# Six gathers ahead in layer 2's mixtures, the loads of x and the sums in one loop, and sequence 0's attention norm behind the first addition

## The chip, the cores and the metric

The kernel runs on one core of one Trainium2 chip. A core has five engines with an instruction queue each: PE (TensorE, matrix products), DVE (VectorE), ACT (ScalarE), POOL (GpSimd) and SP (SyncE, which here only issues transfers). DMAs are issued from the queues of SP, ACT and POOL. An engine works off its queue in order; what one engine needs of another is a semaphore that it waits for. The metric is the device time of one execution in microseconds (us), lower is better. The kernel before was run three times: 1662.7, 1663.09 and 1671.05 us, median 1663.09.

## The reference

A stack of four "macaron" layers on x of 4 sequences x 512 tokens x 128 features, in float32. Each layer adds half of a feed-forward part, then an attention, then half of the same feed-forward part, each on the layer norm of x. Only layer 2 matters here. Its feed-forward part is a mixture of 8 experts in which the experts choose their tokens, and its attention is a linear one:

```python
# feed-forward: n_tok = 2048 tokens, E = 8 experts, k = 256 tokens for each expert
Sm = softmax(xf @ Wr + br)                # (tokens, experts)
G_t, idx_t = top_k(Sm.T, k)               # each expert takes its 256 best tokens
tokens = xf[idx]                          # (256, 8, 128)
mid = silu(einsum('keh,ehf->kef', tokens, W_up[e // 2]) + b_up[e // 2])   # 341 wide
out = einsum('kef,efh->keh', mid, W_down) + b_down
y = zeros_like(xf).at[idx].add(G[..., None] * out)

# attention: q, k = elu(.) + 1, 16 heads of 8
kv = einsum('bshd,bshe->bhde', k, v)
out = einsum('bshd,bhde->bshe', q, kv)
out = einsum('bse,fe->bsf', out.reshape(B, S, E), Wo) + bo

# layer 2
x = x + 0.5 * ffn(norm(x))
x = x + attn(norm(x))
x = x + 0.5 * ffn(norm(x))
```

A token can be taken by several experts, so the results are summed per token.

## The kernel before

x stays in SBUF as 128 partitions x 4 sequences x 4 tiles x 128 features for the whole kernel. Layers 0 to 3 follow each other; layer 2 is the calls `l2_ffn(0)`, `l2_attn()`, `l2_ffn(1)`.

`l2_ffn(k)` (L1165 to L1366), the mixture:

- For each of the 4 sequences it norms x on DVE, transposes the normed tiles on PE, multiplies with the router, and stores x itself to a memory tensor, `sums_of[k, 0]` (L1188, SP's queue). A second tensor, `sums_of[k, 1]`, was filled with zeros long before (`l2_clear`). The results of a token are added to one or the other of these two: they are the two half-sums.
- The normed rows, with the token's 8 probabilities halved behind the 128 features, are stored to memory as `xd` (L1200; the halving is POOL's instruction L1197).
- A search in 15 steps on DVE and PE finds each expert's threshold; then the places of the chosen tokens become the indices `idx` (L1278 to L1295).
- The expert loop. `fetch(e)` (L1304) gathers expert e's 256 rows in two indirect DMAs (h = 0 and 1) from `xd` into tiles `xg`, issued by POOL (L1308). `turn` transposes them on PE (`pt`) and copies them out on DVE (`xTe`, L1322), `up_` multiplies with the up matrix (`pu`) and takes silu on ACT (`mid`), `down` multiplies with the down matrix (`pdn`), adds the bias and scales by the probability on DVE (`y`, L1341 and L1343). Then two indirect DMAs add the two halves of the result to the two half-sums in memory, row by row (L1344, POOL): h = 0 to the first, h = 1 to the second. Two additions to the same half-sum may not overlap, so each waits until the one before it on that tensor has landed.
- The loop is a pipeline over e: `turn(e)`, `up_(e - 1)`, `down(e - 2)`. `AHEAD` experts are fetched before it; from then on `fetch(e)` is placed behind the additions of expert e - `AHEAD`, by a dependence that only orders POOL's queue (L1309 to L1314). `xg` has 16 buffers, one for every gather, `y` has 4, `xTe` and `mid` 3 each.
- At the end, for each sequence, SP loads the first half-sum into x (L1363), ACT's queue loads the second into a tile `yt` (L1362), and DVE adds them (L1366).

`l2_attn()` (L1369 to L1431): `begin(b)` norms sequence b on DVE (four statistics, four aggregates, an inverse root by small instructions on 128x4 numbers, four scalings `xn`), transposes it on PE (`ps`) and copies it out on ACT (`xT`), and adds the output bias to x on POOL (L1386). `project(b)` makes k, v and q with PE, DVE and ACT; `leave(b)` forms the product of keys and values, masks it to the heads on DVE (`kvm`), multiplies it with q (`po`), copies (`oT`, ACT), projects out (`pf`) and adds to x (L1419).

The program is written as loops, and a scheduler places the instructions of each engine into its queue by priorities and expected times; it keeps the data dependences and the added ones. A pool of tiles that is opened where another was closed takes over its memory, and its instructions wait for the last uses of the old tiles.

Of the kernel before, what the change touches and what calls it, by code (L numbers as in the profile page):

```python
# [14 lines left out]
ALU = mybir.AluOpType  # L15
# [5 lines left out]
B, S, D = 4, 512, 128  # L21
# [62 lines left out]
def kernel(  # L84
# [7 lines left out]
    nc = tc.nc  # L92
# [35 lines left out]
    x = res.tile([P, B, TT, D], F32, tag="x", name="x")  # L128
# [5 lines left out]
    def take(t, cols, name):  # L134
        at, n = cols[name]
        return t[:, at : at + n]
# [61 lines left out]
    def over_tiles(row):  # L198
        return row.unsqueeze(1).to_broadcast([P, TT, D])
# [964 lines left out]

    def l2_ffn(k):  # L1165
        W = D + NE
        with tc.tile_pool(name=f"l2f{k}", bufs=1, reuse_waits="tile") as wk:
# [132 lines left out]
            bup = take(pcl, PCOL, "bup")  # L1300
            AHEAD = 4
            xg, xTs, mids, added = {}, {}, {}, {}
# [48 lines left out]
            for e in range(NE + 2):  # L1351
                if e < NE:
                    turn(e)
                if 0 <= e - 1 < NE:
                    up_(e - 1)
                if 0 <= e - 2 < NE:
                    down(e - 2)
                    if e - 2 + AHEAD < NE:
                        fetch(e - 2 + AHEAD)
            for b in range(B):  # L1360
                y = wk.tile([P, TT, D], F32, tag="yt", bufs=B, name=f"yt2_{k}_{b}")
                nc.scalar.dma_start(out=y, in_=sums_of[k, 1][b * S : (b + 1) * S, :].rearrange("(t p) d -> p t d", p=P))  # L1362
                nc.sync.dma_start(  # L1363
                    out=x[:, b], in_=sums_of[k, 0][b * S : (b + 1) * S, :].rearrange("(t p) d -> p t d", p=P)
                )
                nc.vector.tensor_tensor(x[:, b], x[:, b], y, op=ALU.add)  # L1366


    def l2_attn():  # L1369
        with tc.tile_pool(name="l2a", bufs=2, reuse_waits="tile") as wk:  # L1370
# [9 lines left out]

            xTs, qs, ks, vs = {}, {}, {}, {}

            def begin(b):
                xn = layer_norm(wk, x[:, b], f"a2_{b}")
                xTs[b] = transposed(wk, xn, f"a2_{b}")
                nc.gpsimd.tensor_tensor(x[:, b], x[:, b], over_tiles(take(rws, ROW, "bo2")), op=ALU.add)  # L1386

# [32 lines left out]

            begin(0)
            begin(1)
            project(0)
            for b in range(B):
# [432 lines left out]
    for e in range(NE):  # L1857
        t = wexp3.tile([P, N_E3], F32, tag="we3", name=f"we3_{e}")
        nc.sync.dma_start(out=t, in_=e_pack[e * P : (e + 1) * P, :])
        we3.append(t)  # L1860
    l2_ffn(0)
    l2_attn()
    l2_ffn(1)
    early.close()
# [162 lines left out]
```

## Time and profile before

| what | us |
|---|---|
| median of 3 runs | 1663.09 |
| profiled execution, its own time | 1666.47 |
| its span | 1664.7 |
| first mixture, search and indices (from 871.5) to the first gather | 40.9 |
| first mixture, first gather (912.4) to the first addition to memory (926.7) | 14.3 |
| first mixture, first addition to memory to the end of the last one's issue (968.4) | 41.7 |
| loads of x and the half-sum, to DVE's first addition (975.0) | 6.6 |
| attention, first addition to the last L1419 (1016.6) | 41.5 |
| second mixture, first gather (1073.2) to the first addition to memory (1087.7) | 14.5 |
| second mixture, additions to memory (to 1128.9) | 41.2 |
| loads, to DVE's first addition (1135.2) | 6.3 |

The profile is of one execution on the core. Times in its rows are microseconds from the start of the span unless marked ns; "[4.58 <-DVE y L1343]" at the end of a row means that the engine stood idle for 4.58 us before it and that the last thing it waited for was DVE's write of y in line 1343; "issue" is idle time for which the profile shows no releaser. Line numbers are those of the kernel of that profile.

Over the whole span PE is busy 81%, DVE 62%, ACT 40% and POOL 35%. These are averages over stages with different limits, and layer 2 takes about a sixth of the span (from the first mixture's norms at 854 to its last additions into x at 1138).

### The profile page before, as it was taken

How to read it: one execution, taken by the hardware profiler on the slowest of the kernel's cores; microseconds unless marked ns; L12 is line 12 of the kernel's file. 1: busy time of each engine (PE TensorE's matmuls, PEld its weight loads, DVE VectorE, ACT ScalarE, POOL GpSimd, SP SyncE). 2: the span in 40 equal slices, each digit the busy share in tenths (PEclk: the TensorE clock that was granted, in tenths of full speed). 3: DMA queues.
4: the chain of work that ended last, by engine and by line, in shares of the span. 5: the costliest groups of instructions: out<-in, count | busy, mean ns of one | idle time of the engine just before them, and what ended most of it. 6: DMA issues, size and time to landing. Idle time of an engine off the chain costs nothing.

```text
span 1664.7 us, 24721 instructions
## 1 busy us (share of the span) xinstructions
PE 1355.9 (81%) x8372; PEld 849.3 (51%) x8372; DVE 1025.0 (62%) x3179; ACT 668.1 (40%) x1413; POOL 582.6 (35%) x811
## 2 busy tenths in 40 slices
PE   3999899999899987979983646363885899998685
PEld 2898533443698633434552534252784233334685
DVE  4547787787446678888757267625214788883311
ACT  1433477777423323333320212020342377775242
POOL 0354265450255252222210730171784110100585
PEclk9999899999899998989985867585897699998698
DMA  8022212120311010004021221023643422311445
GB/s 322 26 67 59 47 51 64 45 54 17 123 61 49 22 52 1 1 1 190 14 64 30 40 60 53 11 37 82 213 150 100 95 60 57 66 33 28 121 167 183
DMA packets 97144, 121.26 MB, mean 73 GB/s; under 512 B 12223, under 2 KB 85428, under 8 KB 95481
## 3 DMA queue, kind: packets, MB, share of 16 engines
q1 hardware_dynamic: 76393, 69.84, 14.8%
q0 software_dynamic: 15968, 44.98, 9.1%
q10 hardware_dynamic: 4656, 4.86, 0.9%
q8 instruction: 66, 1.08, 0.3%
q14 instruction: 61, 0.50, 0.1%
HBM read 91.88 MB, written 27.79 MB: 72 GB/s over the span
## 4 chain that ended last, share of the span: by engine, by line
PE 64%; DVE 14%; DMA 7%; POOL 6%; issue 5%; SPq 2%; ACT 2%; POOLq 0%; DVEq 0%; ACTq 0%
PE pa L162 9%; PE po L162 7%; PE av L162 7%; PE smax L162 6%; PE sexp L162 6%; PE pc L162 6%; PE pb L162 4%; PE p3b L162 3%; PE lg L162 2%; PE p3a L162 2%; DMA sum<-y,idx 2%; PE p L162 2%; POOL y L1608 2%; PE pq L162 1%; DVE mp L718 1%
## 5 line engine op out<-in xcount | busy, mean ns | idle before, releaser
L718 DVE TENSOR_REDUCE mp<-smax 128x1 f32<-128x512 f32 (+1 forms) x512 | 326.7, 684 | 57.3 <-PE smax L162 56.4
L756 ACT ACTIVATE e<-sexp 128x512 f32<-128x512 f32 x512 | 271.3, 599 | 99.5 <-PE sexp L162 98.4
L162 PE MATMUL smax<-keys,queries 72*128 72x512 bf16 x512 | 200.6, 403 | 11.4 <-DMA queries<-rows_q 4.6
L162 PE MATMUL sexp<-queries,keys 75*128 75x512 bf16 (+1 forms) x512 | 193.1, 388 | 6.2 <-DMA queries<-mT 4.5
L162 PEld LDWEIGHTS <-th 128*128 128x128 bf16 x768 | 74.0, 96 | 97.4 <-issue 4.8
L543 ACT ACTIVATE gl<-pa 128x256 f32<-128x256 f32 x160 | 61.3, 383 | 154.8 <-PE pa L162 115.0
L162 PEld LDWEIGHTS <-queries 72*128 72x128 bf16 x512 | 51.9, 102 | 134.3 <-issue 82.3
L1557 POOL DMA_INDIRECT xg<-xd,src x46 | 46.8, 1018 | 175.3 <-DVE wi L1547 168.1
L544 DVE TENSOR_TENSOR hid<-pa,gl 128x256 f32<-128x256 f32 x160 | 67.3, 422 | 58.7 <-ACT gl L543 58.4
L162 PE MATMUL po<-we,hid 128*128 128x128 f32 x768 | 91.7, 276 | 0.0
L162 PEld LDWEIGHTS po<-we,hid 128*128 128x128 f32 x768 | 90.7, 192 | 1.9
L610 POOL DMA_INDIRECT yg<-y,idx x64 | 66.6, 1040 | 52.5 <-DMA y<-y 42.1
L162 PE MATMUL pa<-ei,we 128*128 128x256 f32 (+1 forms) x352 | 82.7, 390 | 1.5 <-DVE x L910 0.8
L162 PE MATMUL pa<-xTe,we 128*128 128x256 f32 (+1 forms) x352 | 81.8, 381 | 1.0 <-DVE xTe L532 1.0
L162 PEld LDWEIGHTS <-keys 75*128 75x128 bf16 (+1 forms) x512 | 50.2, 100 | 57.7 <-issue 15.5
L162 PEld LDWEIGHTS pa<-ei,we 128*128 128x128 f32 (+1 forms) x352 | 67.1, 196 | 11.5 <-ACT ei L644 1.5
L361 POOL MEMSET paced<- 128x256 f32 x218 | 71.7, 329 | 0.3
L162 PE MATMUL av<-e,v 128*32 128x512 f32 x512 | 70.7, 623 | 0.0
L162 PEld LDWEIGHTS pa<-xTe,we 128*128 128x128 f32 (+1 forms) x352 | 64.6, 189 | 11.8 <-issue 1.4
L162 PE MATMUL av<-e,vp 128*32 128x512 f32 x512 | 68.7, 604 | 0.0
L496 POOL DMA_INDIRECT slots<-xn,idx x32 | 31.4, 982 | 87.7 <-DVE idx L214 82.7
L1308 POOL DMA_INDIRECT xg<-xd,idx x32 | 31.3, 977 | 86.5 <-DVE junk L1289 78.3
(446 smaller groups left out, 2934.8 us busy)
## 6 DMA issues: line engine op xcount, KB each, us to landing
we<-in_w0p_dram SPq DMA_DIRECT2D x8, 1080.0 KB
we<-in_e_pack_dram SPq DMA_DIRECT2D x8, 963.0 KB
queries<-rows SPq DMA_DIRECT2D x48, 96.0 KB
queries<-rows_q SPq DMA_DIRECT2D x48, 96.0 KB
y<-y SPq DMA_DIRECT2D x32, 128.0 KB
xd<-xn_c SPq DMA_DIRECT2D x8, 272.0 KB
slots<-zero ACTq DMA_DIRECT2D x2, 1024.0 KB
xs<-slots SPq DMA_DIRECT2D x16, 128.0 KB
```

Source lines behind the costliest of these rows:

```text
L162: return turn_of(nc.tensor.matmul(*a, **k))
L361: zeros = nc.gpsimd.memset(paced, 0.0)
L496: m = nc.gpsimd.indirect_dma_start(out=slots_of[half][:, :], out_offset=rows_in(idx[:, i, t : t + 1]), in_=xn[:, t, :], in_offset=None, bo ...
L543: nc.scalar.activation(gl, pa[:, 0], AF.Gelu_apprx_tanh)
L544: latest["ins"] = nc.vector.tensor_tensor(hids[e][:, c, :], pa[:, 1], gl, op=ALU.mult)
L610: m = nc.gpsimd.indirect_dma_start(out=yg[:, t, i], out_offset=None, in_=y_d[:, :], in_offset=rows_in(idx[:, i, t : t + 1]), bounds_check= ...
L718: return nc.vector.tensor_reduce(out=self.mp[i][:, t, j], in_=s, axis=AX.X, op=ALU.max, negate=True)
L756: return e, nc.scalar.activation(e, s, AF.Exp, scale=scale)
L1308: m = nc.gpsimd.indirect_dma_start(out=t, out_offset=None, in_=xd[:, :], in_offset=rows_at(e, h))
L1557: m = nc.gpsimd.indirect_dma_start(out=xg[i], out_offset=None, in_=xd[:, :], in_offset=rows_at(src, i), bounds_check=T - 1, oob_is_err=False,)
L1608: m = nc.gpsimd.indirect_dma_start(out=y_d[:, :], out_offset=rows_at(to, i), in_=y, in_offset=None, bounds_check=T - 1, oob_is_err=False,)
```

## The change

Four edits:

- `AHEAD` is 6 instead of 4, in both mixtures: the gathers of six experts stand before the loop, and those of experts 6 and 7 behind the additions of experts 0 and 1.
- The four loads of the half-sum and the four of x are issued in one loop, and DVE's four additions into x follow in a second loop.
- In that second loop, behind each addition, a function `then(b)` is called. For the first mixture it runs the attention's `begin(0)` behind the addition of sequence 0; for the other sequences and for the second mixture it does nothing.
- `begin` moves out of `l2_attn` to the call, with a pool of its own (`l2n`) that is open over the first mixture and the attention, and three buffers for the transposed norm instead of two. In the attention `project(0)` now stands ahead of `begin(1)`.

```diff
-    def l2_ffn(k):
+    def l2_ffn(k, then):
...
-            AHEAD = 4
+            AHEAD = 6
...
+            ys = []
             for b in range(B):
                 y = wk.tile([P, TT, D], F32, tag="yt", bufs=B, name=f"yt2_{k}_{b}")
+                ys.append(y)
                 nc.scalar.dma_start(out=y, in_=sums_of[k, 1][b * S : (b + 1) * S, :].rearrange("(t p) d -> p t d", p=P))
                 nc.sync.dma_start(
                     out=x[:, b], in_=sums_of[k, 0][b * S : (b + 1) * S, :].rearrange("(t p) d -> p t d", p=P)
                 )
-                nc.vector.tensor_tensor(x[:, b], x[:, b], y, op=ALU.add)
-
-
-    def l2_attn():
+            for b in range(B):
+                nc.vector.tensor_tensor(x[:, b], x[:, b], ys[b], op=ALU.add)
+                then(b)
+
+
+    def l2_attn(begin, xTs):
...
-            xTs, qs, ks, vs = {}, {}, {}, {}
-
-            def begin(b):
-                xn = layer_norm(wk, x[:, b], f"a2_{b}")
-                xTs[b] = transposed(wk, xn, f"a2_{b}")
-                nc.gpsimd.tensor_tensor(x[:, b], x[:, b], over_tiles(take(rws, ROW, "bo2")), op=ALU.add)
+            qs, ks, vs = {}, {}, {}
...
-            begin(0)
+            project(0)
             begin(1)
-            project(0)
...
-    l2_ffn(0)
-    l2_attn()
-    l2_ffn(1)
+    with tc.tile_pool(name="l2n", bufs=1, reuse_waits="tile") as pool:
+        xTs = {}
+
+        def begin(b):
+            xn = layer_norm(pool, x[:, b], f"a2_{b}")
+            xTs[b] = transposed(pool, xn, f"a2_{b}", bufs=3)
+            nc.gpsimd.tensor_tensor(x[:, b], x[:, b], over_tiles(take(rws, ROW, "bo2")), op=ALU.add)
+
+        l2_ffn(0, lambda b: begin(b) if b == 0 else None)
+        l2_attn(begin, xTs)
+    l2_ffn(1, lambda b: None)
```

## The prediction

> **What bounds the kernel now.** The spans of the stages come first. The change touches only layer 2, so I read the windows of busy time there; the columns are PE, PEld, DVE, ACT and POOL busy (with instruction counts), granted TensorE clock, DMA share and GB/s.
>
> ```profile
> core 0: us, PE busy (x) PEld busy (x) DVE busy (x) ACT busy (x) POOL busy (x), PEclk, DMA share, GB/s
> 912.40:926.70 14.30, 10.61 (x46) 6.98 (x45) 7.35 (x38) 4.46 (x9) 7.62 (x8) 0.93 0.15 40
> 926.70:968.40 41.70, 24.78 (x123) 20.05 (x121) 8.05 (x25) 7.47 (x17) 33.28 (x24) 0.80 0.31 38
> 975.00:1010.30 35.30, 24.09 (x134) 18.39 (x134) 34.68 (x153) 11.97 (x19) 5.92 (x4) 0.80 0.10 30
> ```
>
> From 926.7 to 968.4 POOL works 33.28 of 41.70 us in 24 instructions, and most of the rest is the 0.30 us between two of them: the expert loop of the first mixture is bound by the issue of indirect DMAs. From 975.0 to 1010.3 DVE works 34.68 of 35.30 us: the attention is bound by DVE. Second, POOL's own instructions in order of time (start, duration, idle before and its releaser): L1308 is a gather, L1344 an addition to memory.
>
> ```profile
> 912.36 1.04 POOL L1308 DMA_INDIRECT xg<-xd,idx  x1 [38.39 <-DVE junk L1289]
> ...
> 921.21 0.94 POOL L1308 DMA_INDIRECT xg<-xd,idx  x1 [0.30 <-issue]
> 926.73 1.64 POOL L1344 DMA_INDIRECT sum<-y,idx  x1 [4.58 <-DVE y L1343]
> 928.68 1.58 POOL L1344 DMA_INDIRECT sum<-y,idx  x1 [0.31 <-DVE y L1341]
> 930.56 1.01 POOL L1308 DMA_INDIRECT xg<-xd,idx  x1 [0.30 <-issue]
> 931.88 0.97 POOL L1308 DMA_INDIRECT xg<-xd,idx  x1 [0.30 <-DMA sum<-y,idx]
> 933.15 1.61 POOL L1344 DMA_INDIRECT sum<-y,idx  x1 [0.30 <-issue]
> ...
> 1113.39 1.61 POOL L1344 DMA_INDIRECT sum<-y,idx  x1 [0.30 <-issue]
> 1115.31 1.58 POOL L1344 DMA_INDIRECT sum<-y,idx  x1 [0.30 <-issue]
> 1117.41 1.55 POOL L1344 DMA_INDIRECT sum<-y,idx  x1 [0.51 <-DVE y L1343]
> 1119.31 1.55 POOL L1344 DMA_INDIRECT sum<-y,idx  x1 [0.35 <-issue]
> 1121.31 1.55 POOL L1344 DMA_INDIRECT sum<-y,idx  x1 [0.44 <-DVE y L1343]
> ```
>
> See three things. POOL stands idle 4.58 us after the eighth gather, until the first expert's result. With two gathers between, one pair of additions follows the next after 933.15 - 926.73 = 6.42 us. Without gathers it follows after 1117.41 - 1113.39 = 4.02 and then 3.90 us. The last is not POOL's own time (2 x (1.55 + 0.30) = 3.70): the half-sums are added to in place, so an addition waits for the one before it on its half. It lands 3.2 to 3.3 us after its start, and some 0.7 us later the next one starts. This is the view of line L1344:
>
> ```profile
> DMA to landing us min/median/max: 3.2/3.3/4.2
> ```
>
> Third, the chain of work that ended last, between the mixture and the attention:
>
> ```profile
> 966.89 3.96 DMA sum<-y,idx
> 970.87 4.08 DMA yt<-sum
> 975.05 0.70 DVE x L1366
> ```
>
> The last addition, then the load of its half-sum, then the first addition into x: whatever makes the last addition earlier moves all behind it.
>
> **The change, part 1: six gathers ahead.** Only the order on POOL changes. The instruction order of the two built kernels shows it: twelve gathers, two additions, two gathers, two additions, two gathers, then twelve additions; before, eight gathers stood first and four pairs stood between additions. In the first mixture gathers run at a pitch of 1.25 us (917.46, 918.71, 919.96, 921.21), so four more after 921.21 end at 921.21 + 4 x 1.25 + 0.94 = 927.15. The indices that they need are written by DVE at 922.34 at the latest, before the twelfth starts (926.21). The first addition goes from 926.73 to 927.15 + 0.30 = 927.45: 0.7 us late. Of the seven steps from first to last pair, four had gathers and three had not: 965.03 - 926.73 = 38.30 us. Now two have gathers (2 x 6.42) and five not (5 x 3.98, the mean of 4.02, 3.90 and 4.03): 32.74 us. The last pair starts 38.30 - 32.74 - 0.72 = 4.8 us earlier. In the second mixture the steps sum to 1125.34 - 1087.73 = 37.61, and the twelfth gather ends at 1082.13 + 5.00 + 0.94 = 1088.07, so the first addition starts at 1088.37, 0.64 late: 37.61 - 32.74 - 0.64 = 4.2 us. Together 9.0 us, all on the chain.
>
> This stands if the results keep ahead of POOL. An expert costs PE about 2.75 us (925.30 to 928.05 from one to the next, when nothing waits), less than 4. Expert 6 is gathered at 931.3 and 932.6 behind the first pair and lands 2.5 us later, at 935.1. Its transposes stand on PE ahead of expert 4's down product, and its copy xTe on DVE ahead of expert 3's scaling: expert 3 is ready at about 937 for a slot at 944, expert 4 at about 939 for 948. Expert 7 lands at 941.4 and frees expert 5 by 945.5 for 952. The four y buffers hold too: the fifth result waits for the first pair, landed at 929.4 + 3.3 = 932.7. At 956.93 in the kernel before, POOL waited 1.03 us for such a result; that wait goes with the late gather.
>
> **Part 2: loads issued together.** I cost this at nothing. Loads of x are on SP's queue and loads of the half-sum on ACT's; in both built kernels the four stand in the same order on each, and before they already went out as 968.21 to 970.2 and 970.87 to 972.9. The second load on ACT gains a wait for POOL, with two loads and the first xT copy queued behind it. What it can wait for stands ahead of it in the program, and the last POOL instruction there that is no DMA ended by 874 (L1197); so it costs nothing.
>
> **Part 3: sequence 0's norm behind the first addition.** DVE's order is new: addition 0, four statistics, four aggregates, addition 1, and so on; before, one statistic stood behind each addition. No DVE work is removed. Pitches from the rows at 975.05 to 982.26 (0.59 for an addition, 0.20 for a statistic, 0.07 for a small instruction, 0.2 where it waits for the one before) put the first scaling 6.4 us behind addition 0 instead of 7.2: 0.8 us earlier. Additions 1 to 3 slip by three statistics and four aggregates, 3 x 0.20 + 4 x 0.07 = 0.9 us, and sequences 1 to 3 with them: sequence 1's scaling comes at about 10.9 instead of 10.7. PE then projects sequence 0 without sequence 1's transposes between. What is late next is the same full DVE: following the new order by these pitches, the second sequence's masked product of keys and values, which leads PE's last fixed stretch, comes between 0.2 us earlier and 0.4 later. One stall can move either way. POOL's bias addition and DVE's two-input instructions collide:
>
> ```profile
> 983.34 0.16 DVE L238 TENSOR_TENSOR ir_t_a<-ir_y_a 128x4 f32<-128x4 f32 x1
> 983.51 1.26 POOL L1386 TENSOR_TENSOR x<-x,rws 128x512 f32<-128x512 f32 x1 [15.07 <-DVE ir_t_a L238]
> 983.62 1.18 DVE L239 TENSOR_TENSOR ir_t_a<-ir_t_a,ir_h_a 128x4 f32<-128x4 f32 x1
> ```
>
> A four-column instruction of 0.13 us elsewhere takes 1.18 us beside it, and 1.23 at 987.02; the two other bias additions, at 992.54 and 1000.78, take 2.00 and 1.40 us themselves and hold no small instruction up. The bounds: if both stalls and DVE's idle 0.6 us go, a gain of 1.05 + 1.09 + 0.6 = 2.7 us; if all four additions stall DVE, a loss of 2.1. I take nothing, midway, since the stage is saturated on both sides of the edit.
>
> The Trainium skill (SBUF — State Buffer, Who interferes with whom) says that a DVE instruction with two SBUF inputs and a GpSimd instruction that reads SBUF exclude each other, the first to start holding the port for its whole length. It speaks against moving a bias addition among DVE's small instructions, and the rows agree with it (1.18 us beside 0.13). By that rule alone, with DVE behind all four, the sum would be 1656.2, the end of the loss.
>
> **Sum.** 4.8 + 4.2 + 0 + 0 = 9.0 us. The profiled execution took 1666.47 us (span 1664.7 and 1.8 around it) and would take 1657.5; it is 3.4 us above the median of the runs, 1663.09. Against the median: 1654.1 us.
>
> **The rivals.**
> - The attention gains. The lead of 0.8 us holds and stalls fall away: up to 2.7 us, 1651.4 to 1653.3. For: DVE held 2.1 us. Against: the same four bias additions remain.
> - The attention loses by more stalls: 1655.1 to 1656.2. For: sequence 0's bias addition again falls among small instructions. Against: two of four did not stall them.
> - Slower: the additions' landing. Twelve in a row, both halves in flight, might land more slowly than behind gathers. Ten ungathered steps count (five per mixture), so each 0.1 us of landing costs 1.0 us; from 4.2 us on (3.25 + 0.9) the gain is gone, at 5.1 it is 1654.1 + 18.5 = 1672.6. For: the last addition of the second mixture took 4.2 us, under the loads of x. Against: all others of the ungathered rows landed in 3.2 or 3.3.
> - Faster: an addition lands before POOL is free, so a step costs POOL's 3.70 us: 10 x 0.28 = 2.8 us more, 1651.3. Against: no ungathered step of the trace is under 3.90. The Trainium skill (DMA: Bandwidth & Descriptors, Anatomy of one DMA — SWDGE (gpsimd) path) fits one such DMA at about 2.0 us plus its bytes over 436 GB/s, an estimate of 2.15 us for 64 KB; the measured 3.2 us disagrees, and the measurement decides.
> - The change does not do what it says: something besides POOL holds the loop, say late results, and the chain keeps most of its length: 1659 to 1663. For: waits on y at 956.93 and 961.04. Against: both follow late gathers.
>
> **How the numbers follow.** The forecast (1653.3 to 1655.1) has 0.60, the attention's gain 0.13, its loss 0.15, slow landing 0.04, fast landing 0.03, no effect 0.05. The range 1650.5 to 1658.0 takes the bounds of the attention and a part of the last case. A change of 0.5%, 8.3 us, is about the least that a measurement of this kernel tells from none; the border is 1654.8, close to the forecast. Faster: most of the forecast's share (0.46), both gains (0.16), together 0.62. Slower by 0.5% needs the slow landing: 0.03. Within: 0.35.
>
> **What would show it.** Right: POOL idle no longer 4.6 but at most 0.4 us ahead of the first addition; it starts 0.6 to 0.7 us after where it stood; 12 additions at the end at 3.9 to 4.1 us a pair; last addition at first gather + 49.8 (before 54.5 and 54.1); attention from addition 0 to the last L1419 (41.5 us before) within 1 us. Wrong: steps above 4.2 us; waits of POOL on y over 0.5 us; a first addition held beyond the twelfth gather; more DVE instructions of over 1 us beside the bias additions; or time gained here given back in layer 3, whose spans (1137.8 to the end) should not change.

## The result and the profile after

The changed kernel's median was 1657.31 us over 7 runs (1652.4 to 1659.61), that of the kernel before 1668.70 over 7 runs (1662.7 to 1675.62). The ratio is 0.9936, with a 95% interval of 0.9914 to 0.9958. The profiled execution took 1654.31 us (span 1652.5), 12.2 us less than that of before.

The forecast was 9.0 us less: 1654.1 us against the first three runs of before, 1659.7 against the median of this comparison, a ratio of 0.9946, which lies inside the interval. That is not to be taken for a confirmation. The two traces can be laid beside each other instruction by instruction, and layer 2, the only stage that is touched, accounts for 5.4 of the 12.2 us:

| stage (us) | before | after | difference | forecast |
|---|---|---|---|---|
| span's start to the first gather of mixture 1 | 912.36 | 909.12 | -3.2 | 0 |
| mixture 1, first gather to the start of the last pair of additions | 52.67 | 49.23 | -3.4 | -4.8 |
| attention, addition 0 into x to the last L1419 | 41.54 | 42.69 | +1.1 | 0 |
| mixture 2, first gather to the start of the last pair | 52.09 | 48.53 | -3.6 | -4.2 |
| the rest of layer 2 (last pair to addition 0, attention to the next first gather) | 76.58 | 77.01 | +0.4 | 0 |
| all of layer 2, first gather to mixture 2's first addition into x | 222.88 | 217.46 | -5.4 | -9.0 |
| from there to the span's end | | | -3.5 | 0 |

The windows of busy time of the changed kernel, for the stages shown of before (columns as there):

```profile
core 0: us, PE busy (x) PEld busy (x) DVE busy (x) ACT busy (x) POOL busy (x), PEclk, DMA share, GB/s
909.15:924.25 15.10, 11.37 (x53) 7.73 (x52) 7.39 (x38) 5.14 (x10) 11.38 (x12) 0.93 0.19 52
924.25:961.95 37.70, 18.65 (x117) 16.18 (x116) 7.60 (x25) 6.50 (x15) 29.12 (x20) 0.82 0.32 36
968.18:1003.48 35.30, 23.72 (x133) 18.62 (x133) 34.27 (x152) 12.01 (x19) 5.60 (x4) 0.79 0.11 31
```

POOL now has 12 instructions ahead of the first addition and 20 behind it, so the second window is 4 us shorter. POOL's own instructions in order of time, in both mixtures:

```profile
909.12 1.04 POOL L1309 DMA_INDIRECT xg<-xd,idx  x1 [38.40 <-DVE junk L1290]
...
923.03 0.94 POOL L1309 DMA_INDIRECT xg<-xd,idx  x1 [0.30 <-DVE y L1342]
924.28 1.64 POOL L1345 DMA_INDIRECT sum<-y,idx  x1 [0.30 <-issue]
...
939.02 1.58 POOL L1345 DMA_INDIRECT sum<-y,idx  x1 [0.30 <-issue]
941.11 1.55 POOL L1345 DMA_INDIRECT sum<-y,idx  x1 [0.50 <-issue]
944.50 1.55 POOL L1345 DMA_INDIRECT sum<-y,idx  x1 [1.84 <-DMA sum<-y,idx]
946.36 1.55 POOL L1345 DMA_INDIRECT sum<-y,idx  x1 [0.31 <-DVE y L1342]
...
1105.97 1.56 POOL L1345 DMA_INDIRECT sum<-y,idx  x1 [0.30 <-DVE y L1342]
1108.89 1.56 POOL L1345 DMA_INDIRECT sum<-y,idx  x1 [1.36 <-issue]
```

The idle 4.58 us ahead of the first addition are gone: it follows the twelfth gather after 0.30. But two additions stand behind idle time that has no counterpart in the working of the prediction, 1.84 us at 944.50 and 1.36 at 1108.89. The time from an addition's start to its landing, from the view of line L1345, has the minimum and the median of before; the longest is 4.3 us where it was 4.2:

```profile
DMA to landing us min/median/max: 3.2/3.3/4.3
```

The chain between mixture and attention has kept its links. They start 6.5, 6.2 and 6.9 us earlier than in the trace of before:

```profile
960.40 4.30 DMA sum<-y,idx
964.72 3.37 DMA yt<-sum
968.18 0.70 DVE x L1370
```

Of the 6.9 us of the last link, 3.2 were there before the first gather.

### The profile page after: what moved, and what is told of

It reads as the page before. It is cut to its first block, busy times and chain, and to the rows that moved or that the text cites. A ratio compares the mean times of both kernels' runs of the same rounds, so it can differ in the third digit from the quotient of the medians.

```text
span 1652.5 us, 24708 instructions
## 1 busy us (share of the span) xinstructions
PE 1339.0 (81%) x8349; PEld 840.4 (51%) x8372; DVE 1023.6 (62%) x3179; ACT 667.8 (40%) x1413; POOL 581.5 (35%) x811
## 3 DMA queue, kind: packets, MB, share of 16 engines
q8 instruction: 66, 1.08, 0.3%
## 4 chain that ended last, share of the span: by engine, by line
PE 60%; DVE 14%; POOL 8%; DMA 7%; issue 5%; SPq 2%; ACT 2%; POOLq 0%; DVEq 0%; ACTq 0%
PE pa L162 9%; PE po L162 7%; PE av L162 6%; PE smax L162 6%; PE sexp L162 6%; PE pc L162 6%; PE pb L162 4%; PE lg L162 2%; POOL y L1607 2%; DVE mp L718 2%; POOL paced L361 2%; POOL xg L1556 2%; PE p L162 2%; PE p3b L162 1%; DMA sum<-y,idx 1%
## 5 line engine op out<-in xcount | busy, mean ns | idle before, releaser
L718 DVE TENSOR_REDUCE mp<-smax 128x1 f32<-128x512 f32 (+1 forms) x512 | 326.0, 682 | 54.1 <-PE smax L162 53.1
L610 POOL DMA_INDIRECT yg<-y,idx x64 | 66.5, 1039 | 52.4 <-DMA y<-y 42.0
L162 PEld LDWEIGHTS pa<-xTe,we 128*128 128x128 f32 (+1 forms) x352 | 64.7, 189 | 11.8 <-issue 1.4
L165 PE MATMUL ps_a<-cst,xn_a 128*128 128x128 f32 x64 | 14.6, 345 | 63.3 <-DVE xn_a L267 62.3
```

The lines of the kernel that those rows point to most:

```text
L162: return turn_of(nc.tensor.matmul(*a, **k))
L165: return turn_of(nc.tensor.transpose(*a, **k))
L610: m = nc.gpsimd.indirect_dma_start(out=yg[:, t, i], out_offset=None, in_=y_d[:, :], in_offset=rows_in(idx[:, i, t : t + 1]), bounds_check= ...
L718: return nc.vector.tensor_reduce(out=self.mp[i][:, t, j], in_=s, axis=AX.X, op=ALU.max, negate=True)
```

## The experiments

The runs were made in four groups and a last pair, each on one chip, with the kernel before timed beside them. One table carries the stages of all; "first addition" and "last pair" are counted from the mixture's first gather, "attention" is addition 0 into x to the last masked product (`kvm`). "Ahead" is the number of experts gathered before the loop. A pair is the two additions of one expert, and a step, below, is the time from the start of one pair to that of the next. Two numbers stand for mixtures 1 and 2. Where no ratio stands, there was one execution only.

| group, kernel | ahead | first addition | last pair | attention | ratio to before (95%) |
|---|---|---|---|---|---|
| before, first profile | 4 | 14.4 / 14.5 | 52.7 / 52.1 | 38.1 | |
| changed, first profile | 6 | 15.2 / 15.2 | 49.2 / 48.5 | 39.2 | 0.9936 (0.9914 to 0.9958) |
| 1 same | 4 | 14.4 / 16.5 | 53.0 / 54.8 | 38.1 | 1.0003 (0.9984 to 1.0023) |
| 1 loads_only | 4 | 14.4 / 16.4 | 52.9 / 54.2 | 38.1 | 1.0011 (0.9990 to 1.0033) |
| 1 norm_only | 4 | 16.4 / 14.6 | 55.3 / 52.3 | 39.6 | 1.0029 (1.0007 to 1.0050) |
| 1 ahead6 | 6 | 15.1 / 16.4 | 49.4 / 50.0 | 38.1 | 0.9964 (0.9938 to 0.9989) |
| 2 bias_pe | 6 | 15.1 / 16.2 | 49.4 / 49.0 | 35.5 | 0.9923 (0.9901 to 0.9945) |
| 2 after_nobias | 6 | 15.2 / 16.3 | 48.6 / 49.2 | 37.2 | |
| 2 shift | 6 | 15.1 / 15.1 | 48.0 / 48.1 | 38.1 | |
| 2 apart | 6 | 15.1 / 16.3 | 46.7 / 47.9 | 38.5 | |
| 3 ahead6_nobias | 6 | 18.2 / 18.1 | 51.4 / 50.7 | 37.3 | |
| 3 best | 6 | 18.2 / 18.1 | 50.8 / 51.8 | 36.3 | 0.9937 (0.9914 to 0.9960) |
| 3 all_ahead | 8 | 24.0 / 23.7 | 52.8 / 51.5 | 35.9 | 0.9966 (0.9946 to 0.9986) |
| 3 after2 (changed) | 6 | 18.2 / 18.2 | 52.0 / 51.8 | 39.3 | 0.9966 (0.9946 to 0.9986) |
| 4 same2 (before) | 4 | 14.4 / 14.4 | 53.3 / 53.1 | 38.1 | 1.0010 (0.9992 to 1.0028) |
| 4 after3 (changed) | 6 | 18.3 / 18.2 | 51.9 / 51.2 | 39.2 | 0.9995 (0.9977 to 1.0014) |
| 4 all_ahead2 | 8 | 24.0 / 23.8 | 53.0 / 52.0 | 35.7 | 0.9980 (0.9962 to 0.9998) |
| 4 best2 | 6 | 18.2 / 18.1 | 51.4 / 52.0 | 36.0 | 0.9960 (0.9942 to 0.9979) |
| 5 ahead5 | 5 | 15.5 / 15.4 | 52.4 / 50.9 | 38.1 | 0.9997 (0.9977 to 1.0016) |
| 5 bias_pe5 | 5 | 15.5 / 16.1 | 51.1 / 51.1 | 35.3 | 0.9964 (0.9942 to 0.9985) |

### What lies outside layer 2: the kernel before, again

No edit.

> The kernel before, unaltered, profiled once more. Between the two profiles shown, 3.2 us of the difference arose ahead of layer 2's first gather and 3.5 us behind its last addition into x, in places that the change does not touch. Theory: that is run-to-run variation of the granted clock, so this profile differs from the first one of before by 1 to 5 us outside layer 2 as well, in a few jumps at places where the clock comes back to full speed, while layer 2 repeats within 1 us (first gather to the last pair of additions 52.7 and 52.1 us, addition 0 to the last masked product 38.1); ratio 1.000 within 0.3%. Rival: stages outside layer 2 are as fixed as layer 2, this profile stands within 1 us of before everywhere, and the 6.7 us belong to the change.

The rival falls. With the same instructions this profile stood 1.8 us ahead of the first one at 60 us and 6.0 us ahead at the first gather; the three profiles of before have their first gather at 912.36, 906.35 and 907.46, the three of the changed kernel at 909.12, 907.70 and 914.88. Between such jumps the rows of two executions agree to hundredths of a microsecond. One jump, in the windows of the first profile of before:

```profile
195.00:200.00 5.00, 5.00 (x44) 2.05 (x42) 1.49 (x3) 2.77 (x7) 0.00 (x0) 0.50 0.03 6
200.00:205.00 5.00, 5.00 (x88) 2.85 (x84) 2.66 (x4) 3.50 (x9) 0.00 (x0) 0.90 0.01 3
```

and of the changed kernel:

```profile
195.00:200.00 5.00, 5.00 (x55) 2.40 (x57) 2.13 (x4) 3.03 (x9) 0.00 (x0) 0.72 0.03 6
200.00:205.00 5.00, 5.00 (x92) 2.69 (x88) 2.54 (x5) 4.52 (x14) 0.00 (x0) 1.00 0.02 5
```

The work is the same, but the granted clock (the third number from the end) comes back to full earlier, and the executions are 1.7 us apart from there to the next jump, at 230 us. So the 6.7 us outside layer 2 are of the size of the difference between two executions of one kernel, and a pair of profiles can only be compared stage by stage.

The theory missed in one place: mixture 2 did not repeat within 1 us but took 2.7 more. Its first addition came at 16.5 instead of 14.5. The window from 6 to 12 us behind the first gather, of this run:

```profile
1073.87:1079.87 6.00, 4.57 (x14) 2.99 (x15) 2.33 (x12) 1.80 (x4) 2.91 (x4) 0.64 0.17 46
```

and of the first profile of before:

```profile
1079.25:1085.25 6.00, 3.98 (x19) 2.73 (x20) 2.33 (x12) 2.32 (x6) 2.91 (x4) 1.00 0.17 46
```

In the slower one TensorE works through the first expert at a clock of 0.64 instead of 1.00. All the first additions at 16.1 to 16.5 in the table have this picture, with a clock of 0.57 to 0.64 in that window. With four experts ahead such a start costs 2.0 us; with six, 1.1 to 1.4, as POOL is busy until 15.1 anyway.

### The parts one by one

Part 1 alone:

```diff
-            AHEAD = 4
+            AHEAD = 6
```

> Part 1 alone: six experts gathered ahead, the loads and the norm as before. Theory: the mixtures take as long as in the changed kernel (first gather to the last pair's start 49.2 and 48.5 us, before 52.7 and 52.1), the attention as long as before (addition 0 to the last masked product 38.1 us), so layer 2 gains 7.0 us and the ratio is about 0.995 to 0.996. The late addition of expert 3 in the first mixture (5.25 us from expert 3's pair to expert 4's where 3.98 was forecast) comes again, since a block of TensorE's code is loaded at the same instruction and holds one DMA engine. Rival on the late addition: it was chance, and the step is 4.0 here. Rival on the attention: the 1.1 us that it lost come from the earlier end of the mixture, so it is 39.2 us here too.

Parts 2 and 3 alone, the changed kernel with

```diff
-            AHEAD = 6
+            AHEAD = 4
```

> Parts 2 and 3 alone: the changed kernel with four experts gathered ahead. Theory: the move of the first sequence's norm costs the attention 1.1 us (addition 0 to the last masked product 39.2 us, before 38.1) by a third stall beside a bias addition and 0.6 us of idle DVE behind transposes; the mixtures take 52.7 and 52.1 us as before; ratio about 1.001. Rival (the prediction): nothing, 38.1 us within 0.3.

Part 2 alone, in the kernel before:

```diff
+            ys = []
             for b in range(B):
                 y = wk.tile([P, TT, D], F32, tag="yt", bufs=B, name=f"yt2_{k}_{b}")
+                ys.append(y)
...
-                nc.vector.tensor_tensor(x[:, b], x[:, b], y, op=ALU.add)
+            for b in range(B):
+                nc.vector.tensor_tensor(x[:, b], x[:, b], ys[b], op=ALU.add)
```

> Part 2 alone: loads in one loop, additions into x in a second, all else as before. Theory and prediction: nothing, 1.000; mixtures 52.7 and 52.1 us, attention 38.1 us. Rival: the second load of the half-sums, which gains a wait for POOL, goes out later than 2.0 us behind the first (before 2.0 us), and each mixture's end is later by as much.

The attention tells the parts apart without doubt: 38.1 us in the profiles with the old order (before, same, loads_only, ahead6, and later shift, same2 and ahead5), 39.2 and 39.6 with the new one, with six experts ahead (39.2) as with four (39.6). So part 3 costs 1.1 us or more, and the rival that it comes from the earlier end of the mixture falls. Part 2 costs nothing that can be seen: the attention is at 38.1, and from the last addition to memory to addition 0 it takes 8.25 and 8.15 us against 8.16 and 7.91 in the first profile of before and 7.78 and 8.43 in the second. Its rival falls: the four loads of the half-sum go out within 2.05 us, before within 2.07. Part 1 gives 3.2 us in the first mixture (49.4 against 52.7); its second mixture began at the low clock. The step from expert 3's pair to expert 4's was 5.48 us, in the place where the changed kernel has 5.25: the late addition is no chance.

### The late addition

Six ahead, and 60 products without a use, four behind each round of the first mixture's search:

```diff
+                if k == 0:
+                    spare = mm_bank([P, 8], f"spare_{i}")
+                    for _ in range(4):
+                        matmul(spare, lhsT=bfc[:, P : 2 * P], rhs=bfc[:, :8], start=True, stop=True)
```

> Six gathers ahead, norms as before, and 60 small products of TensorE without a use in the first mixture's search for thresholds, so that every later block of TensorE's code is loaded some 120 instructions earlier. Theory: the load that held up an addition at 941 (changed kernel) and 944 us (six ahead alone) moves to about 926, where POOL is bound by its own issue; all additions of the first mixture's last four steps follow at 3.9 to 4.1 us (the step from expert 3's pair to expert 4's 4.0 where it was 5.25 and 5.48), and first gather to last pair takes 48.0 us (49.2 and 49.4). Rival: the late addition has another cause at that place, and the step stays above 5 us.

The reason for the theory lies in the DMA view of the changed kernel. A whole addition is 144 packets. This is the addition started at 939.02, from 940.9 to 942.2, with a block of code on queue q8 (66 such blocks, 1.08 MB, in the whole span, one to 253 of TensorE's 16,721 rows, so it is TensorE's):

```profile
DMA packets 136, 0.08 MB, mean 60 GB/s; under 512 B 15, under 2 KB 135, under 8 KB 135
q0 software_dynamic: 135, 0.06, 53.1%
q8 instruction: 1, 0.02, 7.0%
```

and the same view from 942.3 to 943.2:

```profile
DMA packets 9, 0.00 MB, mean 5 GB/s; under 512 B 1, under 2 KB 9, under 8 KB 9
q0 software_dynamic: 9, 0.00, 6.7%
```

135 and 9 are 144, and 9 is the share of one of 16 DMA engines: as the counts suggest, that engine moved the code first and its part of the addition a good microsecond after the others. The next addition to this half waited for it, 944.50 instead of 939.02 + 3.98 = 943.00. With the code moved, POOL's rows in the same place:

```profile
939.33 1.58 POOL L1348 DMA_INDIRECT sum<-y,idx  x1 [0.30 <-issue]
941.39 1.55 POOL L1348 DMA_INDIRECT sum<-y,idx  x1 [0.48 <-issue]
943.41 1.55 POOL L1348 DMA_INDIRECT sum<-y,idx  x1 [0.47 <-issue]
945.47 1.55 POOL L1348 DMA_INDIRECT sum<-y,idx  x1 [0.51 <-issue]
```

The block was loaded at 927 instead of 941, the step is 4.08, and first gather to last pair took 48.03 us, as forecast from the prediction's own steps. The rival falls. The Trainium skill (Runtime: NRT & Kernel Launch, Instruction fetch mechanics) says that an engine's code is refilled in blocks of 16 KiB by a DMA queue that its sequencer drives, and that this is mostly hidden. The blocks agree: 1.08 MB in 66 is 16.4 KB each. The fetch is not hidden from the transfer that shares its DMA engine; no stall of TensorE itself was seen at that place. The 1.36 us in the second mixture coincide with a block of the other code queue (q14, 1106); that one was not tried.

What a step without gathers waits for was tried by sending the odd experts' results to a second pair of sums, which nothing loads:

```diff
+                for h in (2, 3):
+                    y = dram.tile([T, D], F32, tag=f"s{k}{h}", name=f"sum_{k}_{h}")
+                    nc.sync.dma_start(out=y.rearrange("(p n) d -> p (n d)", p=P), in_=zero)
+                    sums_of[k, h] = y
...
-                        out=sums_of[k, h][:, :], out_offset=rows_at(e, h), in_=y[:, h], in_offset=None,
+                        out=sums_of[k, h + 2 * (e % 2)][:, :], out_offset=rows_at(e, h), in_=y[:, h], in_offset=None,
```

> Six gathers ahead, norms as before, and the odd experts' results added to a second pair of half-sums that is not loaded: its output lacks the odd experts of layer 2. Theory: a step without gathers is bound by the landing of the addition before it on the same half; with two steps between, it is bound by POOL's 2 x (1.55 + 0.30) = 3.70 us, and a late landing by a code load is covered too: five steps at 3.7, first gather to last pair 15.1 + 2 x 6.42 + 5 x 3.70 = 46.5 us (49.4 and 50.0). Rival: the results arrive no faster, POOL waits for them, and the steps stay at 3.9 to 4.1.

POOL's rows:

```profile
941.46 1.55 POOL L1348 DMA_INDIRECT sum<-y,idx  x1 [0.30 <-issue]
943.32 1.55 POOL L1348 DMA_INDIRECT sum<-y,idx  x1 [0.30 <-issue]
945.18 1.55 POOL L1348 DMA_INDIRECT sum<-y,idx  x1 [0.30 <-issue]
947.04 1.59 POOL L1348 DMA_INDIRECT sum<-y,idx  x1 [0.30 <-DVE y L1347]
```

Every gap is 0.30 us, the steps are 3.72 to 3.81, and first gather to last pair took 46.67 us (46.5 forecast), with a code load at 942 that harmed nothing. So a step is bound by the landing on its own half-sum, and TensorE and DVE keep ahead of POOL.

### The attention

In the changed kernel three of the four bias additions meet small DVE instructions, in before two did. The rows of POOL and DVE, in order of time:

```profile
975.78 1.26 POOL L1866 TENSOR_TENSOR x<-x,rws 128x512 f32<-128x512 f32 x1 [13.83 <-DVE ir_t_a L238]
975.90 1.17 DVE L239 TENSOR_TENSOR ir_t_a<-ir_t_a,ir_h_a 128x4 f32<-128x4 f32 x1
980.79 1.39 POOL L1866 TENSOR_TENSOR x<-x,rws 128x512 f32<-128x512 f32 x1 [3.75 <-DVE xn_a L267]
981.56 0.63 DVE L244 SCALAR_TENSOR_TENSOR ir_y_a<-ir_t_a,ir_y_a 128x4 f32<-128x4 f32 x1
985.66 1.67 POOL L1866 TENSOR_TENSOR x<-x,rws 128x512 f32<-128x512 f32 x1 [3.49 <-DVE xn_a L267]
986.12 1.23 DVE L244 SCALAR_TENSOR_TENSOR ir_y_a<-ir_t_a,ir_y_a 128x4 f32<-128x4 f32 x1
```

The excess over the usual 0.13 us is 1.04 + 0.50 + 1.10 = 2.6 us, against 1.05 + 1.10 before. The new order's counterpart without POOL (output without that bias):

```diff
-            nc.gpsimd.tensor_tensor(x[:, b], x[:, b], over_tiles(take(rws, ROW, "bo2")), op=ALU.add)
```

> The changed kernel with the bias additions of layer 2's attention left out: its output lacks that bias. Theory: the changed order lost 1.1 us by a third stall of 0.5 us beside a bias addition and by 0.6 us in which DVE waits for a transpose that stands on TensorE ahead of the first sequence's output product. Without the additions the three stalls go (1.04 + 0.50 + 1.09), and addition 0 to the last masked product takes 39.2 - 2.6 = 36.6 us, 0.6 above the 36.0 expected of the old order without POOL. Rival: the stalls are the whole loss, and it takes 36.0 or less.

It took 37.22, above both the 36.6 of the theory and the 36.0 of the rival: by itself the run settled nothing. The old order, six ahead, without the same line:

> Six gathers ahead with the attention's order as before, and the four bias additions left out: the output lacks that bias. DVE runs the same order as with them, so this is the counterpart of the changed kernel without them, which took 37.2 us from addition 0 to the last masked product (39.2 with them). Theory: the old order loses the two stalls, 1.05 + 1.09, and takes 38.1 - 2.1 = 36.0 us; then the new order costs 1.2 us by itself, stalls or none. Rival: the new order costs only by its stalls, and this kernel takes 37.2 as well.

37.29: here the rival was right and my theory wrong. Without the bias additions the two orders take the same, 37.22 and 37.29, and the first masked product comes at 19.9 in the new and 20.3 in the old. The additions cost the old order 38.09 - 37.29 = 0.8 us and the new one 39.24 - 37.22 = 2.0: the difference is the whole loss. The stalls are not worth their length: they sum to 2.1 and 2.6 us. That part of them falls on waits that DVE would have had anyway is a guess.

Taken off POOL for good, by a product with the identity that opens the sum of the output projection:

```diff
-                nc.gpsimd.tensor_tensor(x[:, b], x[:, b], over_tiles(take(rws, ROW, "bo2")), op=ALU.add)
...
                 pf = acc_bank([P, TT, D], f"pf2_{b}")
+                matmul(pf, lhsT=ident, rhs=over_tiles(take(rws, ROW, "bo2")), start=True, stop=False)
                 for t in range(TT):
-                    matmul(pf[:, t, :], lhsT=oT[:, t * P : (t + 1) * P], rhs=take(mat, MAT, "wo2"), start=True, stop=True)
+                    matmul(
+                        pf[:, t, :], lhsT=oT[:, t * P : (t + 1) * P], rhs=take(mat, MAT, "wo2"), start=False,
+                        stop=(t == TT - 1),
+                    )
```

> Six gathers ahead, the attention's norms as before, and the four bias additions taken from POOL to TensorE: a product of the identity and the bias rows opens the sum that the output product adds to. Theory: with no POOL instruction in the attention the two stalls of DVE go (1.18 and 1.23 us where 0.13 is usual), so addition 0 to the last masked product takes 38.1 - 2.1 = 36.0 us; mixtures as in the run with six gathers ahead alone; ratio about 0.995. Rival: the four products of 512 columns (about 0.43 us each, from the up product's 1.30 us for six of half that width and some of less) stand on TensorE ahead of the next sequence's work and the attention stays above 37.5 us.

35.5 us, 2.6 less than before, and a ratio of 0.9923. The scheduler also moved a few instructions on DVE in this kernel, so only 0.8 of the 2.6 can be put down to POOL; the rest is the order that came of it, and was not taken apart.

### The first result held back

The third group was meant to add the gains up: bias on TensorE and the moved code together (the two diffs above), all eight experts ahead with eight result buffers,

```diff
-            AHEAD = 6
+            AHEAD = 8
...
-                y = wk.tile([P, 2, D], F32, tag="y", bufs=4, name=f"y2_{k}_{e}")
+                y = wk.tile([P, 2, D], F32, tag="y", bufs=NE, name=f"y2_{k}_{e}")
```

and the changed kernel once more.

> Six gathers ahead, bias on TensorE, and the 60 small products that move the loads of TensorE's code. Theory: the parts add up: first mixture's gather to last pair 48.0 us (49.4), second 48.0 to 49.5 by the clock at its start, addition 0 to the last masked product 35.5 us; against the run with the bias on TensorE alone 1.4 us less, ratio 0.991 to 0.993. Rival: the products take more from the search's rounds than the load costs, and the first gather of the first mixture comes later than 3 us behind that of the kernels without them.

> Bias on TensorE, all eight experts gathered ahead, and eight result buffers in place of four. Theory: two gathers cost POOL the same 2.5 us ahead of the first addition as between two pairs (6.42 - 3.98 = 2.44), so first gather to last pair is 16 x 1.25 + 0.1 + 7 x 3.98 = 48.0 us, no less than with six ahead (48.0 without a late addition); but the first addition comes at 20.1 us, behind the first result also where the clock is low at the start (16.4 us), so both mixtures take 48.0 to 49.3 us, a code load in the last steps included. Rival: eight results at once leave TensorE idle early, the clock falls, or a step finds its result late: 50 us or more.

> The changed kernel once more, unaltered, beside the others on one chip. Theory: layer 2 repeats (first gather to last pair 49.2 and 48.5, up to 1.3 more where the clock is low at the mixture's start; addition 0 to the last masked product 39.2 to 39.6 us; expert 3's late addition at the same place), while the stages outside differ from the first profile by some us. As it lacks 7.0 - 1.2 us of layer 2 against before, the ratio is 0.996 to 0.997, above the first 0.9936. Rival: the first ratio is the true one, 0.9936, and something outside layer 2 gains 4 us.

All three missed at one point, and in the same way. The first addition came at 18.2 us where the same instructions had 15.2, in every kernel with six ahead and in both mixtures, and at 24 us with sixteen gathers. The parts behind it were as forecast: with the code moved the first mixture's steps were 3.9 to 4.0 (in the second a load now hit one, 5.03), with sixteen gathers the steps were 3.9 to 4.0 but for one of 4.85. The changed kernel's ratio, 0.9966, lay where it was expected although its layer 2 took 223.35 us and not 217.5, so that match was luck.

A further group put the kernels side by side on another chip:

> The kernel before, beside the changed kernel on a chip of their own. Theory: with eight gathers its first addition comes 14.4 us behind the first gather (16.4 where the clock is at half for the first expert), whatever the chip, since a result held until 2 to 3 us behind the last gather (8 x 1.25 + 3 = 13 us) is still in time; ratio 1.000 within 0.3%.

> The changed kernel beside it. In its first profile the first addition came 15.2 us behind the first gather in both mixtures, in its second, on another chip, 18.2 in both, with VectorE and ScalarE starting together some 2.1 us behind the end of the last gather. Theory: that is the chip's doing: here it is one of the two in both mixtures and in all four kernels, and where it is 15.2 to 16.5 the ratio to the kernel before is 0.996 to 0.997 (layer 2 5.4 us shorter, up to 2 us more where before had the clock at half). Rival: it comes and goes from run to run on one chip.

> Bias on TensorE and all sixteen gathers first, which gave a first addition at 24.0 and 23.7 us where 20.1 was expected. Theory: on a chip that holds nothing back it comes at 20.1 us, and first gather to last pair takes 48.0 to 49.3 us (52.8 and 51.5 there); on one that does, again 23.7 to 24.0. Rival: sixteen gathers in a row hold the results on any chip, and it is 23 to 24 us here while the changed kernel has 15.2.

> Six ahead, bias on TensorE, TensorE's code moved. Theory: where the first addition is at 15.1 us, both mixtures take 48.0 us (48.0 to 49.5 with the clock low at the start) and the attention 35.5 to 36.3 us: 4 us less than the changed kernel, ratio to before 0.992 to 0.994.

Again 18.2 and 24 us, and 14.4 in the kernel before. The rows of the changed kernel there, TensorE's down product of the first expert, the last gather, and what follows:

```profile
926.58 1.50 PE L163 MATMUL pdn<-wdn,mid 128*128 128x128 f32 x12
928.81 0.95 POOL L1310 DMA_INDIRECT xg<-xd,idx  x1 [0.30 <-issue]
931.90 0.42 DVE L1343 TENSOR_TENSOR y<-pdn,bdn 128x256 f32<-128x256 f32 x1 [6.79 <-PE pt L166]
931.98 1.19 ACT L1332 ACTIVATE mid<-pu,pcl 128x256 f32<-128x256 f32 x3 [4.56 <-PE pt L166]
933.13 1.64 POOL L1346 DMA_INDIRECT sum<-y,idx  x1 [3.38 <-DVE y L1345]
```

The product stands at its usual place, 11.7 us behind the first gather. DVE, which waits for it, starts at 931.90 instead of 928.1, and ACT, which waits for another product, 0.08 later: 2.1 and 2.2 us behind the end of the last gather. With sixteen gathers it is 2.6 to 2.8 us. I call this the hold. In the first profile of the changed kernel, with the gather's end at 923.97, DVE had started ahead of it:

```profile
922.30 0.42 DVE L1342 TENSOR_TENSOR y<-pdn,bdn 128x256 f32<-128x256 f32 x1 [2.99 <-PE pdn L162]
```

The trace also keeps the semaphore updates, the signals by which one engine learns that another is done, and they show what is late. Counted from the first gather, TensorE's updates in the first mixture of the profile with the hold (after3) come at 11.02, 11.45 and 12.04 us, then none until 17.00, then eight within 0.36 us. Eight of TensorE's rows with an update fall into that gap; they start at their usual places and end, as modelled, at 13.20 to 16.17. In the first profile of the changed kernel their updates came one by one from 13.16 to 16.13. By these records TensorE goes on starting its products in time, and what is late is the news that they are done. All profiles of the last three groups also differ in what they keep: 16,745 to 17,142 updates in all, against 19,588 to 19,659 in the first profiles and the first two groups, and ahead of a first addition behind twelve gathers 47 to 70 of the gathers' 192 landing signals, against 174 to 192. The kernel before is among them (same2, 17,142). Whether the signals were merged on the chip or lost in the record, and whether that and the hold have one cause, no run shows.

Whether the end of the gathers sets it was tried with ten of them:

```diff
-            AHEAD = 4
+            AHEAD = 5
```

> The kernel before with five experts gathered ahead and nothing else. In some profiles the first result was held until 2.1 us behind the end of twelve gathers (2.8 behind sixteen), in others it was not. Theory: where there is a hold it ends 2.1 us behind the last gather whatever their number. Ten gathers end at 0.1 + 9 x 1.25 + 0.9 = 12.3 us, so the first result starts at 14.4 us and the first addition at 15.7 us with a hold, and 13.2 and 14.4 us without. Three steps with gathers and four without follow, 3 x 6.42 + 4 x 3.98 = 35.2 us, and one late addition by a code load of about 1 us: first gather to last pair 50.9 to 51.9 us with the hold, 49.6 to 50.6 without. Rival: the hold begins only behind some ten gathers, and the first addition is at 14.4 us either way.

> The same with the bias additions on TensorE, as a version to set beside both kernels. Theory: mixtures as with five ahead alone, addition 0 to the last masked product 35.5 us; layer 2 5 us less than before with the hold (2 x 1.2 of the mixtures, 2.6 of the attention), 8 us without; ratio 0.995 to 0.997.

```profile
926.42 0.94 POOL L1308 DMA_INDIRECT xg<-xd,idx  x1 [0.30 <-issue]
929.33 0.42 DVE L1341 TENSOR_TENSOR y<-pdn,bdn 128x256 f32<-128x256 f32 x1 [4.18 <-PE pu L162]
930.56 1.64 POOL L1344 DMA_INDIRECT sum<-y,idx  x1 [3.19 <-DVE y L1343]
```

2.0 us behind the last gather's end, the first addition at 15.5: the theory's case with the hold (15.7), and the rival's 14.4 falls. The last pairs were at 52.4 and 50.9 us (50.9 to 51.9 forecast; in the first mixture a code load made one step 5.34), so with a hold five ahead gains next to nothing, 0.9997.

So in some executions what waits for TensorE starts only some 2 us after the last of a row of ten or more gathers. With eight that would be at 11.8 us, ahead of the first result at 13.1, so it would cost nothing; that it is there at all is not shown, as TensorE's updates in same2 come at 10.96, 11.39 and 11.82, where the first profile of before has 10.92, 11.35 and 11.78. With twelve it is at 17.0, the first addition is 3.1 us later, and part 1 gives 1.4 and 2.0 us in the two mixtures (53.3 and 53.1 to 51.9 and 51.2, in the fourth group) instead of 3.4 and 3.6. It was in none of the kernels of the first two groups and in all kernels with ten or more gathers of the last three; the second and the fourth carry the same chip number, so the number does not tell it. What causes it, and why it is there in some executions only, stays open.

## Why the prediction was right or wrong

Three steps of the prediction failed: that results keep ahead of POOL, which cost up to 3.1 us a mixture; "five not (5 x 3.98, ...)", 2.1 us in all; and nothing for part 3, 1.1 us. Of the 9.0 us forecast, layer 2 gave 5.4 where results were in time and 2.7 where they were held.

- **What bounds the mixture: right.** The order on POOL, its pitches and the landing chain hold to a tenth: first addition 0.79 and 0.67 us late (0.72 and 0.64 worked out), steps with gathers 6.39 to 6.43, without 3.9 to 4.1 where nothing else happens. With the code moved the first mixture took 48.03 us; the steps as worked out give 14.4 + 0.7 + 32.7 = 47.8.
- **The sum of part 1, 9.0 us: 7.0 measured.** The step that failed is "five not (5 x 3.98, ...)": one in five was 5.25 in the first mixture and 4.78 in the second, 1.3 + 0.8 us. The first is a late landing by a code load; the second was not tried. The prediction took all ungathered steps for alike, from the three of the second mixture. Four further profiles with four experts ahead (same, loads_only, norm_only, same2) have one such step in their first mixture, 5.0, 4.9, 5.2 and 5.1. The trace that I had in front of me has none over 4.54 there, and that one, the pair at 956.93, waited for a late result, as I read it: DVE's scaling of y ran from 956.37 to 956.85.
- **"This stands if the results keep ahead of POOL": right in the first traces, wrong in others.** This is the step that failed by most. The products are on TensorE when the prediction has them; the overlap failed because their signals came only 2.1 us behind the twelfth gather. The sign named for it, "a first addition held beyond the twelfth gather", is what two later profiles of the changed kernel show, 18.2 instead of 15.2 us. No row of before showed it: there the first result waits for nothing but its product. Why the signals are late stays open.
- **Part 2, nothing: right.**
- **Part 3, nothing: 1.1 us lost.** The pitches were right: first scaling 6.4 us behind addition 0, additions 1 to 3 slipped by 0.7 to 0.9, and without the bias additions the new order is between 0.4 and 0.1 us earlier, as worked out. The step that failed is "One stall can move either way" and "I take nothing, midway": the rival "the attention loses by more stalls" (15%, up to 2.1 us) is what happened. The rule of the Trainium skill that the prediction weighed (SBUF — State Buffer, Who interferes with whom) spoke against this move; the rows agree with it, and the loss is half of what it gave when all four additions were counted.
- **The landing: right in size, one reading wrong.** The prediction held that but for the last addition of the second mixture all ungathered ones landed in 3.2 or 3.3 us. The last of the first mixture took 3.96, in the chain that it shows itself. No sum rests on it, and twelve additions in a row landed as before.
- **Layer 3 should not change: not testable as worded.** Its time, like that of layers 0 and 1, moves by several us between executions of the same kernel.
- **The sum and the measured ratio.** Layer 2 is 5.4 us shorter without the hold (0.9967); with it 222.66 against 225.40 us in the fourth group, 2.7 us (0.9984). The three measured ratios of the changed kernel are 0.9936, 0.9966 and 0.9995. The last two were taken where, by their profiles, the hold was, and their intervals hold 0.9984. The first is some 5 us below 0.9967, which lies just outside its interval; the median of before stood at 1663.09 in its first three runs and at 1668.70 in the seven of that comparison. What made those 5 us was not found, and the agreement of 0.9936 with the forecast rests on them: it is luck.

A version that was faster than both kernels beside it: six ahead with the norm left where it was, the bias on TensorE and the code moved had 0.9960 (0.9942 to 0.9979) beside the changed kernel's 0.9995 (0.9977 to 1.0014) on one chip, medians 1659.68, 1664.95 and 1664.93 for before. The two intervals just touch. In the second group, without the hold, the same without moved code had 0.9923.

## What to carry to other kernels

When a change fills an engine's idle time with more issues, ask what was hidden in that time: here a hold that ends 2 us behind the last gather would cost nothing with eight and cost half of what the six gathers ahead gave with twelve. A chain of landings is only as regular as the DMA engines it shares, and one of its steps in five may cost a third more; read all steps of all stages, not the three of the best one. Where the gain is some tenths of a percent, compare stages, repeat the kernel before, and do not take a matching total for a proof of the working.

## What the runs showed of the hardware that was not expected

- A 16 KB block of TensorE's code, loaded through one DMA engine, delays 9 of an addition's 144 packets, the share of one engine, by about 1.3 us behind the other 135; moving the code by 120 instructions took the step from 5.25 and 5.48 to 4.08.
- In some executions DVE and ACT start what waits for TensorE only 2.0 to 2.8 us behind the end of a row of 10, 12 or 16 gathers, though the product that DVE waits for ends 1 to 9 us earlier in TensorE's rows. In the first mixture of after3, TensorE's semaphore gets no update from 12.04 to 17.00 us behind the first gather and then eight within 0.36 us, while its rows start in time; open why.
- The granted clock changes between 0.50 and 1.00 at moments that differ from one execution to the next. It moved a mixture's first result by 2.0 us; the first gather of layer 2, with the same code ahead of it, lay between 907.70 and 914.88 us in three profiles of the changed kernel.
- The four bias additions on POOL cost 0.8 or 2.0 us of the attention by the DVE instructions that they meet.
